# A four-layer graph network on one core: where the load, reciprocal and division of a tile stand in the output projection

## The chip, the cores and the metric

The kernel runs on one core of a Trainium2 chip. The metric is the device time of one execution in microseconds; the time of a kernel is the median of its runs. The engines are called PE (TensorE, matmul; PEld is its weight load), DVE (VectorE), ACT (ScalarE), POOL (GpSimd) and SP (SyncE, which here only issues DMAs). Each engine works through its own queue in order, and semaphores tie the queues together.

## What is computed

The input is a matrix x of 3327 nodes by 128 features and a weighted adjacency matrix adj of 3327 by 3327, all float32. Four layers follow each other, each with a residual and a layer norm:

```python
x = _layernorm(x + L0(x, adj, adj, Wq, Wk, Wv, Wo))   # attention, see below
x = _layernorm(x + L1(x, adj, W, b))                  # normalised adjacency @ (x W^T + b)
x = _layernorm(x + L2(x, adj, W_in, W_out))           # adj and adj^T, each row-normalised
x = _layernorm(x + L3(x, adj, W, b))                  # x W_self^T + (adj @ x) W_neigh^T + b
```

Layer 0 is where the change lies. It is an attention in which each of the 128 features attends on its own over all nodes, with 8 numbers per node and feature:

```python
q, k, v = [(x @ W.T).reshape(d, n, h) for W in (Wq, Wk, Wv)]
a = softmax(einsum('dnh,dmh->dnm', q, k) * scale + spatial_encoding + edge_encoding, axis=2)
out = einsum('dnm,dmh->dnh', a, v).reshape(n, h * d) @ Wo.T
```

## The kernel before

**Stages.** A first stage projects x to q, k and v and writes them to device memory. The attention loop then takes nearly all the time. It writes its result, not yet divided by the softmax sums, to the array o_s: eight rows of weighted values and a ninth row (index H = 8) with the sum of the exponentials. What is left after it are "the last layers", which work on 26 tiles (T = 26) of 128 nodes; the last has 127.

**The output projection**, the first of these stages, takes for each tile t:

- divide(t): SP loads the tile of o_s into the buffer o (128 nodes x 9 x 128, 576 KB; L1256). DVE takes the reciprocal rec of the ninth part (L1258). POOL multiplies the eight others by it and gives on (L1260); for t = 0 DVE does that.
- heads_turned(t): PE transposes the eight 128 x 128 parts of on (L1268) into banks 0 and 1, four in each, and ACT copies each bank into oT (L1269).
- outputs(t): SP loads the tile xt of x (64 KB; L89, from the helper load_rows). PE sums eight products of oT with Wo (L1277; each counts as two matmul instructions in the trace). DVE adds xt to get h (L1280) and norm() follows: two statistics on DVE (L1192, L1194), a square root on ACT (rstd, L1196), two small operations on DVE (L1197, L1200), and the scaled result x on ACT (L1201).
- turn(t) transposes x on PE (L1211), with a copy to xT by ACT (L1213); support(t) multiplies it by the weights of layer 1 (L1219, two instructions), adds the bias on DVE (lin, L1287) and scales on ACT (y, L1288).

The function stage0(t) writes these for several tiles at a time: heads_turned(t), outputs(t-1), turn of t-3, support(t-4). The loop before the change writes divide(t) and then stage0(t) for each t.

**What sets the order.** The whole block stands in a manual schedule for PE, SP and DVE: these three take their instructions exactly in the order in which the code writes them. ACT and POOL are ordered by the tile framework. The tiles o, rec, on, oT, xt and h come from the pool "work" with three buffers for each name: the fourth tile of a name waits until the first has been read for the last time. So the load of o(t+3) waits for the division of tile t, and on(t+3) waits for the transposes of tile t.

**What follows.** The loop of layer 1 calls gather(t) for each tile: SP loads 1664 KB of the transposed adjacency matrix into a buffer eT (L1236; five buffers), and PE sums 26 products into a bank (L1242, two instructions each). Within gather(0), after its products 2, 7, 12 and 17, stand the last four calls stage0(26) to stage0(29), which finish the outputs, turns and supports of the last tiles. SP's loads for it are written in the same order: the load xt of tile 24 comes in the last step of the loop, then eT of gather(0), then xt of tile 25, then the other eT. Layers 2 and 3 are three more loops of this kind.

Of the kernel before, what the change touches and what calls it, by code (L numbers as in the profile page):

```python
# [45 lines left out]
def spans(n):  # L46

    return [(0, P)] if n == P else [(0, 112), (112, 15)]
# [3 lines left out]
def kernel(ctx: ExitStack, tc: tile.TileContext, x, adj, wq, wk, wv, wo,  # L52
# [18 lines left out]
    T = (N + P - 1) // P  # L71
# [12 lines left out]
    def tokens(t):  # L84
        return P - 1 if t == T - 1 else P

    def load_rows(eng, sb, dram, t):
        for a, n in spans(tokens(t)):
            eng.dma_start(out=sb[a:a + n, :], in_=dram[t * P + a:t * P + a + n, :])  # L89
# [5 lines left out]
    def flat_ap(dram, at, pattern):  # L95

        f = dram.rearrange("r c -> (r c)")
        if isinstance(at, int):
            base = f[at:at + 1]
        else:  # L100
            base = f[ds(at, 1)]
        return bass.AP(base.tensor, base.offset, pattern)
# [1104 lines left out]
    def turn(src, t, b):  # L1207

        n = tokens(t)
        ps = bank(b)  # L1210
        nc.tensor.transpose(ps[:, :n], src[:n, t, :], ident[:n, :n])  # L1211
        xTs[t] = work.tile([P, P], F32, name="xT")
        nc.scalar.copy(xTs[t][:, :n], ps[:, :n])  # L1213
# [8 lines left out]
    def add_columns(t):  # L1222
        part = colsum if t == 0 else small.tile([P, T], F32, name="part")
        nc.vector.tensor_reduce(part, eTs.pop(t), AX.X, ALU.add)
        if t:
            nc.vector.tensor_tensor(colsum, colsum, part, ALU.add)
# [3 lines left out]
    def gather(t, y, col, b, meanwhile=()):  # L1230


        n = tokens(t)
        todo = list(meanwhile)
        e = big.tile([P, T, P], F32, tag="big", name="eT")
        nc.sync.dma_start(out=e.rearrange("p s n -> p (s n)"), in_=adjT_s[t * P:(t + 1) * P, :])  # L1236
        ps = bank(b)
        for s in range(T):
            while todo and todo[0][0] <= s:
                todo.pop(0)[1]()  # L1240
            m = tokens(s)
            nc.tensor.matmul(ps[:n, 0:D], lhsT=e[:m, s, :n], rhs=y[:m, s, col:col + D],  # L1242
                             start=(s == 0), stop=(s == T - 1))
        for _, what in todo:
            what()
        eTs[t] = e
        return ps
# [4 lines left out]
    def divide(t):  # L1252
        n = tokens(t)
        o = work.tile([P, A1, D], F32, name="o")
        for a, k in spans(n):
            nc.sync.dma_start(out=o[a:a + k], in_=flat_ap(o_s, (t * P + a) * D, [[D, k], [SLOTS, A1], [1, D]]))  # L1256
        rec = work.tile([P, D], F32, name="rec")
        nc.vector.reciprocal(rec[:n, :], o[:n, H, :])  # L1258
        ons[t] = work.tile([P, H, D], F32, name="on")
        (nc.gpsimd if t else nc.vector).tensor_tensor(ons[t][:n], o[:n, 0:H, :], rec[:n, :].unsqueeze(1).to_broadcast([n, H, D]), ALU.mult)  # L1260

    def heads_turned(t):
        n = tokens(t)
        oTs[t] = work.tile([P, H, P], F32, name="oT")
        for c in range(0, H, 4):
            ps = bank(c // 4).rearrange("p (c n) -> p c n", n=P)
            for i in range(4):
                nc.tensor.transpose(ps[:, i, :n], ons[t][:n, c + i, :], ident[:n, :n])  # L1268
            nc.scalar.copy(oTs[t][:, c:c + 4, :n], ps[:, :, :n])  # L1269

    def outputs(t):
        n = tokens(t)
        xt = work.tile([P, D], F32, name="xt0")
        load_rows(nc.sync, xt, x, t)
        ps = bank(2 + t % 2)
        for c in range(H):
            nc.tensor.matmul(ps[:n, 0:D], lhsT=oTs[t][:, c, :n], rhs=woT[:, c * D:(c + 1) * D],  # L1277
                             start=(c == 0), stop=(c == H - 1))
        h = work.tile([P, D], F32, name="h0")
        nc.vector.tensor_tensor(h[:n, :], ps[:n, 0:D], xt[:n, :], ALU.add)  # L1280
        norm(n, h[:n, :], xs[0][:n, t, :], True)

    def support(t):
        n = tokens(t)
        ps = project(t, w1T, 5)
        lin = work.tile([P, D], F32, name="lin")
        nc.vector.tensor_tensor(lin[:n, :], ps[:n, 0:D], b1_sb[:n, :], ALU.add)  # L1287
        nc.scalar.mul(y1[:n, t, :], lin[:n, :], dinv[:n, t:t + 1])  # L1288

    def messages(t):  # L1290
        n = tokens(t)
        ps = project(t, w2, 5)
        nc.scalar.copy(y2[:n, t, :], ps[:n, 0:2 * D])
# [9 lines left out]
    with tc.manual_schedule(engines={mybir.EngineType.PE, mybir.EngineType.SP, mybir.EngineType.DVE}):  # L1303
        def stage0(t):
            if t < T:
                heads_turned(t)
            if 1 <= t <= T:
                outputs(t - 1)
            if 3 <= t <= T + 2:
                turn(xs[0], t - 3, 4)  # L1310
            if 4 <= t <= T + 3:
                support(t - 4)

        for t in range(T):
            divide(t)
            stage0(t)


        def after(src, t, finish):
            return [(12, lambda: turn(src, t, 4)), (19, lambda: finish(t))] if t >= 0 else []  # L1320

        for t in range(T):
            n = tokens(t)
            ps = gather(t, y1, 0, 6 + t % 2,
                        after(xs[1], t - 1, messages) if t else
                        [(2 + 5 * k, lambda k=k: stage0(T + k)) for k in range(4)])
            z = work.tile([P, D], F32, name="z")
            nc.vector.tensor_tensor(z[:n, :], ps[:n, 0:D], y1[:n, t, :], ALU.add)
            h = work.tile([P, D], F32, name="h")
            nc.vector.scalar_tensor_tensor(h[:n, :], z[:n, :], dinv[:n, t:t + 1], xs[0][:n, t, :],  # L1330
                                           ALU.mult, ALU.add)
            norm(n, h[:n, :], xs[1][:n, t, :])
            add_columns(t)
        inv_col = inverse_degree(colsum, "inv_col")


        backT = act.tile([P, NP], F32, name="backT")
        cols = [(c, min(512, N - c)) for c in range(0, N, 512)]
        order = [6, 0, 1, 2, 3, 4, 5]
        acc = {}  # L1340
        for t in range(T):
            n = tokens(t)
            a = big.tile([P, T * P], F32, tag="big", name="a2")
            load_rows(nc.sync, a[:, 0:N], adj, t)
            for i, (c, w) in enumerate(cols):
                if t == 0 and i == 3:
                    turn(xs[1], T - 1, 4)
                if t == 0 and i == 5:
                    messages(T - 1)
                if t == 0:  # L1350
                    acc[i] = bank(order[i])
                nc.tensor.matmul(acc[i][:, 0:w], lhsT=y2[:n, t, D:2 * D], rhs=a[:n, c:c + w],  # L1352
                                 start=(t == 0), stop=(t == T - 1))
        for i, (c, w) in enumerate(cols):
            copy(i, backT[:, c:c + w], acc[i][:, 0:w])


        for t in range(T):
            n = tokens(t)
            zs = {}  # L1360

            def back(t=t, n=n):
                pb = bank(t % 2)
                nc.tensor.transpose(pb[:n, 0:P], backT[:, t * P:t * P + n], ident)  # L1364
                zs[t] = work.tile([P, D], F32, name="z")
                nc.vector.scalar_tensor_tensor(zs[t][:n, :], pb[:n, 0:D], inv_col[:n, t:t + 1], xs[1][:n, t, :],
                                               ALU.mult, ALU.add)

            ps = gather(t, y2, 0, 7 - t % 2, [(6, back)] + after(xs[0], t - 1, last_inputs))
            h = work.tile([P, D], F32, name="h")  # L1370
            nc.vector.scalar_tensor_tensor(h[:n, :], ps[:n, 0:D], inv_row[:n, t:t + 1], zs[t][:n, :],  # L1371
                                           ALU.mult, ALU.add)
            norm(n, h[:n, :], xs[0][:n, t, :])


        for t in range(T):
            n = tokens(t)
            ps = gather(t, y3, 0, 6 + t % 2, after(xs[0], T - 1, last_inputs) if t == 0 else ())
            h = work.tile([P, D], F32, name="h")
            nc.vector.tensor_tensor(h[:n, :], ps[:n, 0:D], xs[1][:n, t, :], ALU.add)  # L1380
            res = work.tile([P, D], F32, name="res")
            norm(n, h[:n, :], res[:n, :])
            store_rows(nc.gpsimd, out, res, t)
# [29 lines left out]
```

## Time and profile before

| | |
|---|---|
| median of 3 runs | 10696.29 us (10695.95 to 10702.73) |
| the profiled execution | 10692.01 us, its span 10689.9 us |
| mean granted clock of TensorE | 0.987 |
| attention loop, about 300 to 9772 us of the span | 9472 us |
| output projection, 9784.0 to 10042.7 us | 258.7 us |
| gathers of layer 1, 10042.7 to 10210.9 us | 168.2 us |
| the two stages of layer 2, to 10523 us | 312 us |
| last gathers, to the end | 167 us |

The profiled execution is one run; its span goes from the first to the last instruction, and 2.1 us of its time lie around the span. The page lists for each group of instructions the line, the engine, the operation, the output and inputs with their shapes, the count, the busy time with the mean of one, and the idle time of the engine before it with what ended it. These are the largest groups of the output projection on each engine, asked for the stretch from 9784 to 10043 us:

| line | engine | count | mean ns of one | idle before, us | ended by |
|---|---|---|---|---|---|
| L1268 transposes | PE | 200 | 428 | 128.8 | POOL on 114.6, DMA of o 14.2 |
| L1277 outputs | PE | 400 | 396 | 0.0 | |
| L1258 rec | DVE | 25 | 943 | 3.6 | DMA of o |
| L1280 h | DVE | 25 | 292 | 191.1 | PE L1277 |
| L1260 on | POOL | 24 | 2340 | 210.7 | DVE rec 175.3 |
| L1269 oT | ACT | 50 | 586 | 99.3 | PE L1268 |

The duration of a matmul in such a row holds its way through the array; matmuls overlap, so counts times means are more than the time that PE is occupied. From one transposes' group to the next in steady state there are about 10.2 us, and the loads of o land 2.6 to 6.1 us after they are issued (median 3.3).

### The profile page before, as it was taken

To read this page: it belongs to the slowest core of one execution; us is meant where nothing else is said; L and a number is where in the kernel's file an instruction comes from. 1 tells how busy PE (TensorE), PEld (TensorE's weight loads), DVE (VectorE), ACT (ScalarE), POOL (GpSimd) and SP (SyncE) were. 2 spreads that over 40 slices of the span, in tenths; PEclk is the share of its full clock that TensorE was granted. 3 is DMA by queue.
4 is the path that set the end of the run, shared out by engine and by line. 5 is a ranking of instruction groups with operands and counts; after the bars stand their busy time and mean duration, and the time that the engine had idled before them with its cause. 6 is when DMAs were issued, how large, how long until landed. Compare 5 with 4: busy or idle time off the path is not lost. (4 is left out here: it accounts for less than half of the span.)

```text
span 10689.9 us, 209547 instructions
## 1 busy us (share of the span) xinstructions
PE 10435.8 (98%) x76835; PEld 4092.9 (38%) x76835; DVE 9107.7 (85%) x16616; ACT 9455.6 (88%) x11231; POOL 1626.1 (15%) x2733
## 2 busy tenths in 40 slices
PE   8999999999999999999999999999999999997799
PEld 5333333333333333333333333333333333333779
DVE  6789998899988999889998899989999889995422
ACT  3899999999999999999999999999999999996200
POOL 0211221111111112111121110111111210001100
PEclk9999999999999999999999999999999999998899
DMA  7678996789977899778897688976889768885486
GB/s 270 187 187 195 214 219 181 183 195 210 214 183 182 195 208 216 180 181 196 207 216 188 176 190 202 205 181 169 201 204 214 191 166 191 194 197 136 159 294 249
DMA packets 1013939, 2117.12 MB, mean 198 GB/s; under 512 B 206566, under 2 KB 731118, under 8 KB 999088
## 3 DMA queue, kind: packets, MB, share of 16 engines
q1 hardware_dynamic: 932054, 1985.62, 75.8%
q0 software_dynamic: 79136, 116.02, 3.6%
q8 instruction: 621, 10.17, 0.4%
q14 instruction: 408, 3.33, 0.1%
q10 hardware_dynamic: 1720, 1.97, 0.1%
HBM read 1863.16 MB, written 239.54 MB: 197 GB/s over the span
## 5 line engine op out<-in xcount | busy, mean ns | idle before, releaser
L743 ACT ACTIVATE e<-sc 128x952 f32<-128x952 f32 (+2 forms) x10752 | 9227.1, 992 | 246.2 <-PE sc L738 174.6
L778 PE MATMUL o<-e,v_pad 128*32 128x476 f32 (+1 forms) x46592 | 5664.4, 573 | 9.6 <-POOL v_pad L552 7.3
L738 PE MATMUL sc<-qt,kt 64*128 64x476 f32 x23296 | 4311.8, 436 | 44.2 <-DVE ey L632 22.0
L738 PEld LDWEIGHTS sc<-qt,kt 64*128 64x128 f32 x23296 | 2132.2, 184 | 4267.1 <-ACT e L743 2589.3
L642 DVE SCALAR_TENSOR_TENSOR e<-e,ey 128x476 f32<-128x476 f32 x4116 | 2655.1, 652 | 36.4
L632 DVE TENSOR_SCALAR ey<-sc 128x476 int32<-128x476 f32 x2058 | 1340.5, 651 | 592.1 <-ACT e L743 557.1
L778 PEld LDWEIGHTS o<-e,v_pad 128*32 128x32 f32 (+1 forms) x46592 | 1032.4, 108 | 1923.0 <-issue 1894.4
L552 POOL COPY v_pad<-vs 128x192 f32<-128x192 f32 (+1 forms) x896 | 545.0, 631 | 7741.7 <-DMA vs<-v_img 6231.5
L642 DVE SCALAR_TENSOR_TENSOR e<-ey 128x476 f32<-128x476 f32 x2058 | 1339.3, 654 | 28.3
L642 DVE SCALAR_TENSOR_TENSOR e<-e,et 128x476 f32<-128x476 f32 x2058 | 1340.0, 654 | 7.6
L639 DVE TENSOR_SCALAR ey<-ey 128x476 int32<-128x476 int32 x2058 | 838.9, 410 | 13.9
L636 DVE TENSOR_SCALAR et<-ey 128x476 int32<-128x476 int32 x2058 | 841.3, 412 | 11.0
L242 POOL DMA_DIRECT2D adjT_s<-at x1352 | 751.8, 564 | 158.4 <-DMA adjT_s<-at 118.5
L1242 PE MATMUL bank<-y,eT 128*128 128x128 f32 (+1 forms) x4056 | 470.6, 275 | 0.4 <-DVE h L1371 0.4
L1242 PEld LDWEIGHTS bank<-y,eT 128*128 128x128 f32 (+1 forms) x4056 | 467.5, 192 | 3.3 <-DVE h L1371 0.6
L1196 ACT ACTIVATE rstd<-mv,eps 128x1 f32<-128x1 f32 x104 | 30.6, 294 | 276.8 <-DVE mv L1194 276.8
L538 DVE CAST qt<-qt 64x1904 fp32r<-64x1904 f32 x224 | 259.1, 1157 | 7.4
L792 DVE TENSOR_TENSOR acc<-o,acc 128x476 f32<-128x476 f32 x231 | 151.0, 654 | 105.0 <-PE o L778 103.2
L536 DVE TENSOR_SCALAR qt<-qt 32x1428 fp32r<-32x1428 f32 x224 | 201.0, 897 | 21.0 <-DMA qt<-q_s 15.4
L800 POOL DMA_DIRECT2D o_s<-acc x304 | 185.2, 613 | 16.5 <-issue 9.1
L1268 PE MATMUL bank<-ident,on 128*128 128x128 f32 (+1 forms) x208 | 51.1, 427 | 133.7 <-POOL on L1260 119.5
L1280 DVE TENSOR_TENSOR h<-bank,xt 128x128 f32<-128x128 f32 (+1 forms) x26 | 7.6, 292 | 191.8 <-PE bank L1277 191.8
(142 smaller groups left out, 2475.9 us busy)
## 6 DMA issues: line engine op xcount, KB each, us to landing
qt<-qimg SPq DMA_DIRECT2D x1344, 476.0 KB
kt<-k_s SPq DMA_DIRECT2D x5316, 96.0 KB
kt<-k_s SPq DMA_DIRECT2D x1762, 128.0 KB
eT<-adjT_s SPq DMA_DIRECT2D x78, 1664.0 KB
qimg<-qt SPq DMA_DIRECT2D x224, 476.0 KB
vs<-v_img SPq DMA_DIRECT2D x224, 224.0 KB
adjT_s<-at POOLq DMA_DIRECT2D x1352, 32.0 KB, 5.0
vs<-v_img SPq DMA_DIRECT2D x224, 192.0 KB
```

The source lines that it names most:

```text
L242: nc.gpsimd.dma_start(out=flat_ap(adjT_s, (t * P + 32 * q) * NP + c * PIECE, [[NP, 32], [P, ns], [1, P]]), in_=at[32 * i:32 * i + 32].rear ...
L536: return [(0.9, lambda: nc.vector.tensor_scalar(qt[32:64, 1:], qf[0:32, 0:GROUP - 1], -1.0, None, ALU.mult)), (0.42, lambda: nc.vector.ten ...
L538: (1.17, lambda: nc.vector.tensor_copy(qt[64:128], qf[0:64]))]
L552: nc.gpsimd.tensor_copy(vp[:, 32:32 + nt * GROUP * 32].rearrange("p (x c) -> p x c", c=32)[:, :, 0:H], vs.rearrange("p (x c) -> p x c", c=H))
L632: nc.vector.tensor_scalar(yi, x, -58 * math.log(2.0), 2 ** 24 / math.log(2.0), ALU.max, ALU.mult)
L636: nc.vector.tensor_scalar(parts["t"].bitcast(I32), yi, UPPER, EXPONENT, ALU.bitwise_and, ALU.bitwise_xor)
L639: nc.vector.tensor_scalar(yi, yi, LOWER, QUARTER, ALU.bitwise_and, ALU.bitwise_or)
L642: nc.vector.scalar_tensor_tensor(e, e if i else y, POLY[i], parts["t"] if i == len(POLY) - 1 else y, ALU.add, ALU.mult)
L738: nc.tensor.matmul(s[:, i, 0:CW], lhsT=kt[64 * rg:64 * rg + 64, k, pos * P:(pos + 1) * P], rhs=qt[64 * rg:64 * rg + 64, k, :], start=False ...
L743: nc.scalar.activation(e[:, 0:own, :], s[:, 0:own, 0:CW], AF.Exp, bias=-2 * PHASE, scale=2.0)
L778: nc.tensor.matmul(o[32 * j:32 * j + 32, 0:CW], lhsT=values[b, g][:m, c:c + 32], rhs=es[b, g * GROUP + j, r][:m, :], start=first and u == ...
L1242: nc.tensor.matmul(ps[:n, 0:D], lhsT=e[:m, s, :n], rhs=y[:m, s, col:col + D], start=(s == 0), stop=(s == T - 1))
```

## The change

The calls of divide are moved. Those for tiles 0 and 1 stand ahead of the loop, and each step t then writes divide(t+2), as long as there is such a tile, in front of stage0(t). The functions themselves are not touched; buffers, engines and the number of instructions stay as they are.

```diff
-        for t in range(T):
-            divide(t)
+        for t in range(2):
+            divide(t)
+        for t in range(T):
+            if t + 2 < T:
+                divide(t + 2)
             stage0(t)
```

With it the order on DVE in step t becomes: reciprocal of tile t+2, then h and the norm of tile t-1, then lin of tile t-4. On SP the load of o of tile t+2 comes ahead of the load xt of tile t-1. The division on POOL stays with its reciprocal.

## The prediction

> **What bounds the kernel now.** I read the windows by stage first, to see where the change lies and what it can touch.
>
> ```profile
> 300.00:9772.00 9472.00, 9407.56 (x70615) 3242.32 (x70615) 8629.00 (x15711) 9227.13 (x10752) 1519.90 (x2633) 1.00 0.82 194
> 9784.00:10042.70 258.70, 136.57 (x675) 131.23 (x676) 55.85 (x170) 62.87 (x146) 58.50 (x25) 0.66 0.33 100
> 10042.70:10210.90 168.20, 167.86 (x1457) 166.34 (x1456) 136.87 (x214) 27.62 (x88) 0.00 (x0) 1.00 0.67 244
> ```
>
> The columns are the stretch, its length, then busy time of PE, PEld, DVE, ACT and POOL, the granted clock, the DMA share and GB/s. The attention loop (first line) keeps PE busy for 99% of the time; the change leaves it alone. In the output projection (second line, 258.7 us for 26 tiles) no engine is full: PE 53%, ACT 24%, POOL 23%, DVE 22%, and the granted clock is 0.66. The first gather behind it (third line) is all PE at clock 1.00. So only the second line can move by much, and latency bounds it. The chain of waits at its end shows the ring:
>
> ```profile
> 10024.91 2.34 POOL on L1260
> 10027.30 1.97 PE bank L1268 x8
> 10029.26 3.05 PE bank L1277 x16
> 10034.07 0.95 DVE rec L1258
> 10035.14 2.35 POOL on L1260
> 10037.53 1.96 PE bank L1268 x8
> 10039.49 3.05 PE bank L1277 x16
> 10042.87 0.45 PE bank L1242 x4
> ```
>
> The columns are start, length, engine and line. The division of tile t, its eight transposes, the sixteen matmuls of tile t-1, and only then the reciprocal of tile t+1. Why must that reciprocal wait for matmuls of another tile? The timeline of one step answers:
>
> ```profile
> 10001.62 0.29 DVE L1280 TENSOR_TENSOR h<-bank,xt 128x128 f32<-128x128 f32 x1 [7.57 <-PE bank L1277]
> ...
> 10003.15 0.28 DVE L1287 TENSOR_TENSOR lin<-bank,b_sb 128x128 f32<-128x128 f32 x1
> ...
> 10003.35 0.94 DVE L1258 RECIPROCAL rec<-o 128x128 f32<-128x128 f32 x1
> ...
> 10004.42 2.34 POOL L1260 TENSOR_TENSOR on<-o,rec 128x1024 f32<-128x1024 f32 x1 [7.90 <-DVE rec L1258]
> 10006.79 0.96 SPq L1256 DMA_DIRECT2D o<-o_s  x2
> 10006.81 0.51 PEld L1268 LDWEIGHTS bank<-ident,on 128*128 128x128 f32 x3 [5.09 <-POOL on L1260]
> ```
>
> DVE works in the written order: h, which waits 7.57 us for PE, and the normalisation stand ahead of rec. PE then sits 5.09 us until the division is done. From rec to rec is 10.24 us (10023.83 to 10034.07). The load is not what is late: o is issued 0.03 us after the division three tiles earlier ends, and DVE waited for it 3.6 us in all.
>
> **Nothing is added or removed, only moved.** The same 27 load issues, 26 reciprocals and 26 multiplies are issued, two tiles earlier. Per queue:
>
> *DVE.* rec(t+2) (0.94 us) now stands before h(t-1). What it needs is old: o(t+2) is loaded into the buffer that on(t-1) released. When PE reaches step t, on(t) is ready, so PE's 5.09 us of waiting and the ring go. What is late next? PE's own work, if the clock rises. At clock 1.00 a gather matmul takes 0.1116 us (4.24 us for 38 in the chain). A step has 8 transposes, 16 matmuls of outputs, 1 turn and 2 of support: 27 x 0.1116 = 3.01 us. The others per step: DVE 2.67 us (h at 10022.10 to the end of rec at 10024.77, with its 0.36 us wait for ACT); ACT 2 x 0.586 + 0.266 + 0.294 + 0.492 + 0.385 = 2.61; POOL 2.34 plus 0.05 of handing over = 2.39; SP two issues, 0.7. A ring remains that runs over two steps: h to the end of y is 2.43 us (10022.10 to 10024.53), two copies of oT 1.17 if ACT takes them behind y, half the transposes 0.45, sixteen matmuls 1.79, landing some 0.25: 6.1 us, 3.05 a step. With a few handovers I take 3.2.
>
> *The clock.* Here the estimate hangs on the granted clock. In 10006.82 to 10009.60 it was 0.50 with PE busy, and in the 1.5 us from 10010.60 it was 0.77, so it rose after about 4 us of work; in the gathers it stays at 1.00, and in the first 300 us, with PE busy for 86%, it was 0.94. With PE busy for 3.0 of 3.2 us I take 1.00. If it stayed low, a step would be as 9821.59 to 9827.37, turn and support included, 5.8 us less some rise at its end: 5.5.
>
> The Trainium skill (TensorE: Matmul & The Clock Gate, What's actually happening) says that the clock doubles after one busy window of about 3.4 us and that windows run freely, not from the first matmul. The trace agrees: 5.4 us at 0.50 in 9790.30 to 9795.70, about 4 us in the later step. By that rule steps after the first run at full clock, as in my sum; by the mean 0.66 of the row they would not.
>
> *SP.* o(t+2) now stands in front of xt(t-1), and waits for the end of on(t-1). That division lies some two steps before h(t-1) needs xt; xt's other wait, h(t-4), is older still. At the start xt(0) falls behind o(2) and o(3); o(3) waits for on(0) until 9786.4, so xt(0) lands by 9792.9 (longest landing of an o, 6.1), before h(0) at 9795.73. Cost nothing; were it late, h(0) would wait a few us once. Behind xt(24) and xt(25) hang the tiles eT of the gather. Their lead shrinks: eT(0) goes out when h(21) is done, three steps or 9.6 us ahead of the gather (10012.84 now, 30 us ahead). The windows show its traffic from 10013 to 10018.5, so 5.7 us cover it, and the next four came at 4 us each (433 GB/s) against 6.35 us that a gather tile takes. Nothing, or at worst 5.7 us once.
>
> *DMA.* A step moves 576 + 64 KB = 655,360 bytes; at the 284 to 314 GB/s seen while o is loaded that is 2.1 to 2.3 us. It fits in 3.2. From on(t-1) to on(t+2) the ring of three o buffers is 3.3 (median landing) + 0.95 + 2.39 = 6.6 us, 2.2 a step.
>
> *POOL beside DVE.* Until now on ran while DVE was all but idle (2339 to 2344 ns); now it runs beside rec, h and lin. No row shows that pair. The nearest, the POOL copy of the attention (L552), takes 342 ns at least and 518 in the median beside a busy DVE. Bounds: 2.39 a step, or POOL and DVE taking turns: 2.39 + 2.37 of DVE's busy time = 4.76. I take 2.39, since it has 0.8 us of room, and keep 4.76.
>
> The Trainium skill (SBUF — State Buffer, Who interferes with whom) has VectorE and GpSimd block each other through a shared port pair when the VectorE operation has two SBUF inputs or a two-port mode. h and lin read one input from PSUM and rec has one input, so by that rule on stays at 2.34; by turns a step costs 4.76. No run here shows it.
>
> **The sum.** Tile 1's division still ends at 9790.26, and outputs(0) at 9795.70, as now. on(2) follows on(1) and ends by 9793.6, so the first step that gains, t = 2, starts at 9795.70. Twenty-four steps of 3.2 us and 1.2 us for a slow first step or a wait at the gather: 9795.7 + 76.8 + 1.2 = 9873.7, where the gather's first matmul now starts at 10042.70. Gain 169.0. The profiled execution took 10692.0 us (span 10689.9), so 10523.0; the median of the runs is 4.3 above it: 10527. What follows is bound by PE at clock 1.00 and only shifts.
>
> **Rivals.** (1) POOL and DVE take turns: 24 x 4.76 + 9795.7 + 1.2 = 9911.1, gain 131.6, so 10565. For it: L552's spread. Against: no DVE row in the step is long except rec. (2) ACT, whose order is not written out here, takes rstd(t-1) behind the next step's copies of oT. Then from h it is 0.9 (transposes) + 0.3 + 1.17 + 0.3 + 0.7 to lin, and 0.95 for rec: 4.3 us a step, gain 142.6, so 10554. Against: in the timeline rstd, x and y follow in the written order. (3) The clock stays low: 5.5 us, gain 113.8, so 10583. Against it the rows above. (4) The change does not take effect, because a buffer comes free later than I read it: 10696. Against: o is issued 0.03 us after the division three tiles back. (5) Slower: rec(t+2), ahead of h(t-1) on DVE, waits for a late load and holds the normalisation, and behind it support and PE. The ring of three o buffers then sets the step, (L + 3.34) / 3 for a landing of L. It passes 10.24 us from L = 27.4, and is slower by 0.2% (21 us over 24 steps) from L = 30; at L = 36 a step is 13.1 and the time 10765. For it: the share of the DMA engines is 1.15 in the rush at 9790. Against: the longest landing there is 6.1 us.
>
> **How the numbers follow.** The forecast, a step of 3.0 to 3.9 us, has 0.77; its own range is 10514 (a step of 3.01 without the 1.2 gives 10521.5, less the 6.8 us by which the runs spread) to 10544. The rivals have 0.06 (turns), 0.06 (ACT's order), 0.04 (clock), 0.04 (no effect) and 0.03 (slower). The range, 10514 to 10568, takes in the first two and leaves out the others, 0.11, and some tails. A measurement of this kernel can tell about 0.2%, or 21 us, from no change: faster 0.93, same 0.04, slower 0.03.
>
> **What would show it.** In the profile after: the projection lasts some 90 us at clock near 1.00; from rec to rec 3.0 to 3.9 us; the wait of PE for on (119.5 us in 25 times) falls under 10; DVE's wait for L1277 falls from 191 to under 40; on stays at 2.34; the gathers keep their lengths. I am wrong if on stretches, if PE's clock stays at 0.5 to 0.7, if rec waits for o in each step, or if the first gather waits for eT by more than 6 us.

## The result and the profile after

The changed kernel takes 10520.22 us (median of 4 runs, 10515.31 to 10524.45) against 10697.1 us before (4 runs, 10695.95 to 10702.73): the ratio is 0.9833, with a 95% interval of 0.9816 to 0.985. That is 176.9 us less; 10527 was predicted, with 10514 to 10568 as the range.

The windows of the profile after (stretch, length, busy time of PE, PEld, DVE, ACT and POOL, granted clock, DMA share, GB/s):

```profile
9787.40:9803.50 16.10, 6.95 (x32) 6.58 (x33) 6.34 (x12) 3.85 (x6) 5.82 (x3) 0.50 0.97 253
9803.50:9875.20 71.70, 71.70 (x646) 71.65 (x646) 50.86 (x164) 52.02 (x140) 53.11 (x23) 1.00 0.83 233
9875.20:10043.50 168.30, 167.96 (x1457) 166.34 (x1456) 136.92 (x215) 27.57 (x88) 0.00 (x0) 1.00 0.76 279
```

The first line is the start, from the first load of o to the transposes of tile 2. The second line is the other 24 steps: PE is busy in all of its 71.7 us, at clock 1.00. The third is the first gather, 168.3 us as before. From the first load of o to the first matmul of the gather it took 263.1 us before (9779.6 to 10042.7) and takes 87.8 us now (9787.4 to 9875.2), which is 175.3 us less. So the whole gain lies in the projection. In this profile the attention loop ended 8 us later than in the one before. It is the same code, and the runs of the kernel before spread by 22 us over all comparisons made here (10686.9 to 10708.8).

The chain of waits in the same stage (start, length, engine and line):

```profile
9840.28 1.79 PE bank L1277 x16
9842.40 0.87 PE bank L1268 x8
9843.28 1.79 PE bank L1277 x16
9845.40 0.87 PE bank L1268 x8
9846.27 1.79 PE bank L1277 x16
9848.39 0.87 PE bank L1268 x8
```

DVE and POOL are gone from the chain. From transposes to transposes it is 2.99 us, and the 0.33 us between a line's end and the next start are turn and support. In this chain the transposes take 0.87 us where they took 1.97, the sixteen matmuls 1.79 where they took 3.05. One step in the timeline:

```profile
9836.12 0.29 DVE L1280 TENSOR_TENSOR h<-bank,xt 128x128 f32<-128x128 f32 x1 [0.33 <-PE bank L1277]
...
9837.00 0.29 ACT L1196 ACTIVATE rstd<-mv,eps 128x1 f32<-128x1 f32 x1 [0.49 <-DVE mv L1194]
...
9837.20 1.05 ACT L1269 COPY oT<-bank 128x512 f32<-128x512 f32 x2
...
9837.85 0.94 DVE L1258 RECIPROCAL rec<-o 128x128 f32<-128x128 f32 x1
9838.14 0.50 ACT L1201 ACTIVATE x<-h,off,rstd 128x128 f32<-128x128 f32 x1
9838.31 0.36 SPq L1256 DMA_DIRECT2D o<-o_s  x1
...
9838.92 2.36 POOL L1260 TENSOR_TENSOR on<-o,rec 128x1024 f32<-128x1024 f32 x1 [0.64 <-DVE rec L1258]
```

DVE still takes rec behind h and its norm. But this rec belongs to a tile whose transposes come two steps later, and the wait of h for PE has shrunk from 7.57 to 0.33 us. The waits of the stage say the same (who waited for whom, us in all, times, longest):

```profile
POOL on L1260 <- DVE rec L1258: 12.4, 18, 1.6
...
DVE h L1280 <- PE bank L1277: 9.1, 20, 1.9
DVE rec L1258 <- DMA o<-o_s: 8.3, 5, 3.2
...
PE bank L1268 <- POOL on L1260: 2.1, 1, 2.1
```

PE waited once for a division, 2.1 us at the start, where it had waited 25 times for 119.5 us in all.

### The profile page after: what moved, and what is told of

Same layout as the page of the kernel before. It is cut to its first block, busy times and chain, and to the rows that moved or that the text cites. A ratio compares the mean times of both kernels' runs of the same rounds, so it can differ in the third digit from the quotient of the medians.

```text
span 10522.3 us, 209548 instructions
## 1 busy us (share of the span) xinstructions
PE 10377.1 (99%) x76835; PEld 4037.7 (38%) x76835; DVE 9110.6 (87%) x16616; ACT 9449.2 (90%) x11231; POOL 1612.1 (15%) x2733
## 3 DMA queue, kind: packets, MB, share of 16 engines
q10 hardware_dynamic: 1720, 1.97, 0.1%
## 5 line engine op out<-in xcount | busy, mean ns | idle before, releaser
L1355 PE MATMUL bank<-a,y 128*128 128x512 f32 (+2 forms) x364 | 145.5, 561 | 0.0
L354 ACT ACTIVATE hi<-pp 128x1024 fp32r<-128x1024 f32 x52 | 53.1, 1025 | 89.2 <-PE pp L300 87.5
```

## The experiments

The theory: before, one ring ran through DVE's order (h and norm, rec, division, transposes, outputs, next h), and the waits in it also kept the clock of PE low; with the reciprocal two tiles ahead the ring is open and PE's own 27 instructions set the step. For each kernel the table gives its time, the ratio to the kernel before in the same comparison, and from its profile the length from the first load of o to the gather, the usual step and the granted clock of the stage from about 9800 us on.

| kernel | time, us | ratio (95% interval) | projection, us | step, us | clock |
|---|---|---|---|---|---|
| before | 10697.1 | | 263.1 | 10.24 | 0.66 |
| changed | 10520.2 | 0.9833 (0.9816 to 0.985) | 87.8 | 2.99 | 1.00 |
| loads alone ahead | 10696.5 | 0.9997 (0.9988 to 1.0007) | 260.3 | 10.24 | 0.66 |
| one tile ahead | 10554.2 | 0.9863 (0.9847 to 0.988) | 116.2 | 4.06 | 0.96 |
| before, PE kept busy | 10653.1 | 0.9955 (0.9938 to 0.9972) | 215.6 | 8.12 | 1.00 |
| changed, more PE work | 10548.1 | 0.9858 (0.9842 to 0.9875) | 113.7 | 4.11 | 1.00 |
| before, division on DVE | 10646.9 | 0.9954 (0.9937 to 0.9971) | 204.8 | 6.96 to 8.55 | 0.85 |
| changed, division on DVE | 10544.9 | 0.9856 (0.9839 to 0.9872) | 105.0 | 3.83 | 1.00 |
| before, division on DVE, PE kept busy | 10626.5 | 0.9935 (0.9919 to 0.9952) | 186.9 | 6.97 | 1.00 |

**Is it the load or the reciprocal?** divide is cut in two, fetch (the load) and the rest, and only fetch moves:

```diff
...
+        for t in range(2):
+            fetch(t)
         for t in range(T):
+            if t + 2 < T:
+                fetch(t + 2)
             divide(t)
             stage0(t)
```

> Only the loads of o stand two tiles ahead on SP; reciprocal and division stay in front of step t. Theory (the ring runs through DVE's order, and loads were never late: DVE waited 3.6 us for them in all): the step stays at 10.2 us and the time at 10692 to 10704. Rival (the earlier load is what pays): a step near 3 us and a time near 10520.

The time did not change. The timeline of this kernel shows why an earlier load could not help:

```profile
10004.62 2.34 POOL L1264 TENSOR_TENSOR on<-o,rec 128x1024 f32<-128x1024 f32 x1 [7.90 <-DVE rec L1262]
10006.99 0.96 SPq L1256 DMA_DIRECT2D o<-o_s  x2
```

The load goes out when a division ends and frees its buffer (10006.96 here), wherever its call is written; POOL still waits 7.90 us for rec. The place of the load is not the cause.

**Is one tile enough?** The call becomes divide(t + 1), with divide(0) ahead of the loop.

```diff
+        divide(0)
         for t in range(T):
-            divide(t)
+            if t + 1 < T:
+                divide(t + 1)
             stage0(t)
```

> The whole of divide stands one tile ahead instead of two. Theory: rec(t+2) comes behind h(t-1) and its norm, and the transposes of t+2 wait for its division; from the rows of the changed kernel h to rec 1.73 us, to the start of on 1.07, on 2.36, then 2.97 us from the transposes to the h of the next tile, 8.1 us in all for two steps, so a step of 4.1 us in place of 2.99 and a time 24 x 1.1 = 26 us over the changed kernel, 10546. The clock stays at 1.00. Rival (it is enough that the reciprocal is ahead at all): 2.99 us a step and 10520.

The projection is 28.4 us longer than with two tiles, where 26 were expected; the time is 34 us more, with the spread of the runs in it. The clock did not stay at 1.00 all the time, as had been expected: near the start it fell to 0.50 twice (9809.8 to 9813.2 and 9820.0 to 9823.5), and two of the first four steps took 7.09 and 6.84 us in place of about 5. From there on it was 1.00. In the profile every other division starts at 9866.78, 9874.90, 9883.02: 8.12 us for two steps, for 8.1 expected. So the ring is still closed, but it runs over two steps, and its wait stands in its waits:

```profile
POOL on L1260 <- DVE rec L1258: 27.9, 11, 4.6
...
PE bank L1268 <- POOL on L1260: 22.1, 12, 2.6
```

In every second step PE waits for a division. Two tiles ahead are needed, not just "ahead".

**How much is the clock?** The order of before, with matmuls of the identity where PE waits:

```diff
+        def warm(count):
+            ps = bank(7)
+            for _ in range(count):
+                nc.tensor.matmul(ps[:, 0:P], lhsT=ident, rhs=ident, start=True, stop=True)
         for t in range(T):
             divide(t)
             stage0(t)
+            warm(20)
```

> The order of before, with 20 extra matmuls of the identity (40 instructions) into an unused bank at the end of each step, where PE waits some 5 us; their result is not used. Theory (part of the 10.24 us was the clock at 0.50): the clock stays at 1.00, the ring is 1.73 + 1.07 + 2.36 + 2.97 = 8.1 us a step, so 24 x 2.1 = 50 us less than before, 10647. Rival (the clock is a symptom and does not matter): 10697, or more, since the extra matmuls stand in front of the transposes.

The ratio 0.9955 is 48 us, the projection is 47.5 us shorter and the step 8.12 us. PE does 40 instructions more in each step and the step is 2.1 us shorter. So with the ring closed the clock is worth 2.1 of the 7.25 us that the change takes from a step; the other 5.1 come when the ring is opened at full clock. No run has an open ring at the low clock, and in that order the split could be another.

**Does PE set the step now?** The changed order, with five such matmuls behind each step:

```diff
...
         for t in range(T):
             if t + 2 < T:
                 divide(t + 2)
             stage0(t)
+            warm(5)
```

> The changed order, with 5 extra matmuls of the identity (10 instructions, 1.12 us at clock 1.00) per step into an unused bank; their result is not used. Theory (PE's own work now sets the step): the step goes from 2.99 to 4.1 us, 26 x 1.12 = 29 us over the changed kernel, 10549. Rival (a ring through ACT and DVE sets the step, with PE only nearly full): less than 10 us over it.

The projection grew by 25.9 us and the time by 28; the step is 4.11, the old 2.99 and the 1.12 us of the ten instructions. Nothing took any of it up, so PE sets the step. The ring of 3.05 us a step that the prediction kept beside PE's 3.01 does not bind.

**Is the division a link of the ring?** Every division on DVE in place of POOL, in the order of before:

```diff
-        (nc.gpsimd if t else nc.vector).tensor_tensor(ons[t][:n], ...)
+        nc.vector.tensor_tensor(ons[t][:n], ...)
```

> The order of before, with every division on DVE behind its reciprocal (1.23 us as tile 0 has it) instead of on POOL. Theory (the division is a link of the ring): the step loses 2.34 + 0.12 of handing over and gains 1.23, so 10.24 becomes 9.0, 25 x 1.24 = 31 us less, 10666. Rival (the division lies beside the ring, and only the reciprocal's place counts): 10697.

It is a link, but the size was wrong: 52 us by the medians and 58.3 in the projection, for 31 expected. The starts of h are not even: 9870.26, 9878.82, 9885.78, 9892.74, 9900.99. The windows of these four steps, in the columns of the first fence:

```profile
9870.30:9878.80 8.50, 5.03 (x29) 4.76 (x29) 3.40 (x8) 2.52 (x6) 0.00 (x0) 0.77 0.27 77
9878.80:9885.80 7.00, 3.22 (x30) 3.06 (x29) 3.45 (x9) 2.42 (x6) 0.00 (x0) 1.00 0.27 78
9885.80:9892.70 6.90, 3.12 (x29) 2.96 (x28) 3.40 (x8) 2.42 (x6) 0.00 (x0) 1.00 0.33 90
9892.70:9901.00 8.30, 4.52 (x29) 4.36 (x29) 3.44 (x9) 2.42 (x6) 0.00 (x0) 0.83 0.37 97
```

The same 29 or so instructions of PE take 3.1 to 3.2 us in two of the steps and 4.5 to 5.0 in the others, and the granted clock goes with them. I had left the clock of before in the sum. To settle it, the order of before with both edits:

```diff
-        (nc.gpsimd if t else nc.vector).tensor_tensor(ons[t][:n], ...)
+        nc.vector.tensor_tensor(ons[t][:n], ...)
...
             stage0(t)
+            warm(15)
```

> The order of before with both changes of the two runs before it: every division on DVE, and 15 extra matmuls of the identity (30 instructions) per step into an unused bank, whose result is not used. The division on DVE alone gained 52 us where 31 were expected, its steps in the profile are 6.96 us twice and then 8.25 and 8.55, and its clock is 0.85 in the mean. Theory (the surplus is the clock: the shorter wait lets it stay high in half of the steps): with PE kept busy all steps are 6.96 us and the clock is 1.00, so 25 x (10.24 - 6.96) = 82 us less than before, 10617. Rival (the surplus comes from POOL's handover being dearer than I read it, and the clock has nothing to do with it): the steps stay uneven, and the time stays near 10647.

All steps are 6.97 us and the clock is 1.00, as the theory has it. The time is 66.9 us below the kernel before of the same comparison and the projection 76.2 us shorter, for 82 expected. Part of the rest is in the timeline: the extra matmuls behind tile 0 ran at half clock and held the transposes of tile 1 to 9807.31, and the last ones stand 3.4 us in front of the gather.

**Should the division leave POOL?** The changed order, with every division on DVE:

```diff
-        (nc.gpsimd if t else nc.vector).tensor_tensor(ons[t][:n], ...)
+        nc.vector.tensor_tensor(ons[t][:n], ...)
```

> The changed order, with every division on DVE. Theory (nothing waits for the division any more, and what counts is each engine's work per step): DVE has 2.67 + 1.23 + 0.05 = 3.95 us and takes over from PE, 24 x 0.96 = 23 us over the changed kernel, 10543. Rival (a shorter division still helps): 10520 or less.

Slower than the changed kernel, by 24.7 us in time and 17.2 in the projection; the step is 3.83 us. DVE, busy for 73.0 us of the 84 between 9806 and 9890, is now the bound, and PE waits for it:

```profile
PEld bank L1219 <- DVE lin L1287: 18.0, 20, 2.5
PE bank L1219 <- DVE lin L1287: 13.3, 20, 2.3
```

So the same edit gains about 50 us where the division is in the ring and loses about 25 where it is not. None of these kernels is faster than the changed one.

## Why the prediction was right

**The bound before.** The chain, the 7.57 us wait of h and the 5.09 us of PE were read as one ring through DVE's order. The loads moved alone show that it was not the load, and two tiles against one tile show that the ring has to be opened by two steps.

**The size.** The term that was off is the step: 3.2 us with "a few handovers", measured 2.99 (71.7 us for 24). The 27 matmul instructions at 0.1116 us, 3.01, were the step itself; nothing had to be added. That makes 24 x 0.21 = 5.0 us, and the allowance of 1.2 us for a slow step or a wait at the gather was not used either. Together these are 6.2 of the 6.3 us by which the projection (87.8 us) was shorter than the sum had it (94.1 from the first load). The gain of the medians, 176.9 us for 169.0 forecast, is off by 1.6 us more, which the spread of the runs covers. The start was sized rightly: tile 2 began 16.1 us after the first load of o in the sum and in the trace.

**The clock.** Taken as 1.00 and measured 1.00 from 9804.1 on. The kernel before with a busy PE shows what it is worth in the old order, 48 us. The Trainium skill (TensorE: Matmul & The Clock Gate, What's actually happening) has the full clock come after one busy window of about 3.4 us; the trace agrees, with 0.50 up to 9804.1 and 1.00 behind it, 5.6 us after PE's work became dense at 9798.5.

**The rivals.** POOL and DVE do not take turns: on runs beside rec and h and takes 2358 ns in the median (2342 to 2376), against 2340 before. The Trainium skill (SBUF — State Buffer, Who interferes with whom) has the two engines block each other only when the VectorE operation has two SBUF inputs or a two-port mode; on was never longer by more than 36 ns, which agrees. ACT's order did change: the timeline above has the two copies of oT between rstd and x. That delays x, not rstd, and nothing waits for x within the step. Loads were late only at the start: rec waited 8.3 us for o in 5 of 26 cases, 8.1 of it in the first four, and the first h still waited for PE. In those first 16 us the loads of o and of the weights shared the DMA engines (share 0.97). The eT tiles came in time, since the first gather keeps its length; eT(0) went out 8.2 us ahead of it, for 9.6 forecast.

## What to carry to other kernels

When no engine is full in a stage, look for a ring: an operation whose place in an in-order queue is behind the wait of another tile. Write it as many steps ahead as the ring has steps, here two, which is also what three buffers allow, and look at each other queue that it passes. Where PE waits for about 2 us or more in each step (the shortest wait here behind which the clock fell was 2.15 us, and behind waits of 1.8 us it held), count its matmuls twice, once at the clock of the trace and once at full clock: the gain from an open ring includes the clock, and so may the gain from any edit that only shortens the wait.

## What the runs showed of the hardware

I had not expected the clock to come and go with a period of its own. With the division on DVE in the old order all steps hold the same work, and PE waits 3.5 to 3.8 us in each of the four steps shown above; the clock stayed at 1.00 through two steps of 6.96 us and was 0.77 and 0.83 in the two longer ones. Read in slices of 0.1 us, this profile has the clock change between 0.50 and 1.00 at 9867.4, 9870.8, 9874.2 and 9877.6, and next at 9898.1: the distances are 3.41 us or a multiple of it. So they are in the profile before (9816.7, 9820.2, 9827.0, 9830.4) and with one tile ahead (9809.8, 9813.2, 9820.0, 9823.5).

Cut into stretches of 3.41 us at these points, the three profiles agree on what moves the clock. It fell behind every stretch in which PE was busy for 1.32 us or less, transposes counted, and held where PE was busy for 1.45 us or more. It rose behind stretches with 3.06 us or more and stayed at 0.50 with 2.53 or less.

The Trainium skill (TensorE: Matmul & The Clock Gate, What's actually happening) has windows of 3.4 us that run freely and puts the drop behind an idle one. The distances agree with it; the drop does not, since the clock fell behind stretches that were not idle.

The step of 10.24 us before is three times 3.41 us, and the four uneven steps together, 30.7 us, are nine times. The steps came down to 10.24 from 10.44 in the kernel before, and up to it from 9.77 with the loads alone ahead, so the step seems to settle on a multiple of this length. No run tests that.
